# A graph-network layer on one core: B's rows beside zeros, TensorE alone waits for the gathers, and six more groups taken from GpSimd

## The chip, the core and the metric

The kernel runs on one core of a Trainium2 chip. The time is device microseconds of one launch; the median of three runs of the kernel before is 3400.61 us (3400.22 to 3402.1). The engines are called as in the profile: PE (TensorE, with PEld for its weight loads), DVE (VectorE), ACT (ScalarE), POOL (GpSimd) and SP (SyncE, which here only issues transfers).

## What is computed

One message-passing layer with 12500 nodes of 128 features and 400000 edges with 32 features, sorted by their target node:

```python
h = jnp.maximum(_layernorm(x), 0.0)
m = relu(concat([h[src], h[dst], ea]) @ w1 + b1) @ w2 + b2       # 400000 edges
agg = jax.ops.segment_sum(m, dst, num_segments=12500)
gi = agg @ w_ih + b_ih ; gh = h @ w_hh + b_hh                    # a GRU cell
out = x + (1 - z) * n + z * h
```

## The kernel before

w1 has three parts, so an edge's hidden value is relu(A[src] + B[dst] + ea @ w1c) with A = h @ w1a and B = h @ w1b + b1 made once per node. A and B are tables in DRAM; h stays transposed in SBUF (hT_all). The sum over edges is taken before w2, which is folded into the gates.

The edges lie in tiles of 128. Eight tiles are a group k (391 groups; tile j of half a has number a * 4 + j), and a group is worked in two units u = 2k and u = 2k + 1. Because the edges are sorted by target, the targets of a group lie in two windows of V = 32 nodes, the second SHIFT = 8 nodes after the first.

For a group the kernel needs:

- **G**, the rows A[src] of its 1024 edges: 8 indirect gathers of 128 rows each on POOL (`gather`, L156), into one of GBUFS = 11 buffers. The first RAW = 9 groups gather x instead of A.
- **L**, the left side of a product: one-hots of the targets on 64 partitions and the edge features on the other 64. `fetch` (L563, L566) brings it for two groups at a time by two transfers on SP, six groups ahead, into three buffers; DVE makes the one-hots in place (L575).
- **RW**, the right side: rows 0 to 31 hold the first window's 32 rows of B in the left 128 columns, rows 32 to 63 the second window's in the right 128; the rest of these rows is zeros, written once. Below lies w1c. `window_rows` (L602) brings it by two transfers on SP, four groups ahead, into four buffers.
- **pre** = L times RW on PE (L673), B[dst] + ea @ w1c; **RB** = relu(pre + G) on DVE in one instruction (`add`, L701); **OH**, one-hots of the edges' targets in their window, on DVE (`onehot`, L623); and **seg**, PE's products of OH and RB, which sum the edges of a window (L724).

**Groups without a gather.** POOL does not gather all groups. `SPREAD` names how many groups each other engine takes, and spreads them evenly. On ACT and DVE a group's columns of h are copied one by one out of hT_all: on ACT 1024 copies (L960), on DVE 512 instructions that take two columns each (L967) with 8 copies that put them in order (L972); PE then multiplies by w1a, and ACT makes RB by a relu (L710) instead of DVE's add. On SP a group's 1024 rows of A are fetched by 1024 transfers of 512 bytes into the buffer G_sp (L952). Each engine first loads addresses into registers (L945): 16 at a time on ACT, 32 on DVE and SP. A job is cut into steps (4 rows on SP), and `run_jobs` puts them evenly among the units between the job's start and its end; on SP the first starts at u = 24, a job ends at 2k - 8, and the next starts at 2k + 2.

**Order.** The program is written out by hand and every engine works in that order (`manual_schedule`). In one turn of u: new gathers, for an even u the next window's rows and for every second group the next L, then `stages(u)`, which runs several units ahead: one-hots of the group three ahead, `pre(u + 3)`, `add(u + 2)`; then `seg(u)`. Steps of the jobs are put between (`other`). All transfers of SP stand in one queue in program order; they use eight semaphores in turn, so that a transfer is issued only when the eighth before it has landed.

Every 14 groups (BLOCKS) a block of nodes goes through the GRU gates (`node`), and `batch_product` and `batch_store` make and store the next 448 rows of B.

Of the kernel before, what the change touches and what calls it, by code (L numbers as in the profile page):

```python
# [9 lines left out]
F32 = mybir.dt.float32  # L10
F16 = mybir.dt.float16
I32 = mybir.dt.int32
U8 = mybir.dt.uint8
# [39 lines left out]
PIECE = 128  # L53
STEP = {"act": 4, "dve": 8, "sp": 4}
ROW = 4 * D
SPREAD = {"dve": 27, "act": 28, "sp": 2}
START = {"dve": 14, "act": 4, "sp": 24}
NR = 12672

# [4 lines left out]
def tile_gnn(ctx: ExitStack, tc: tile.TileContext, x, src, srcT, dstT, dstP, eaT, eaP, w1, b1, w2T, b2,  # L64
# [69 lines left out]
    A = dram.tile([N, D], F32, name="A")  # L134
    stats = dram.tile([N, 2], F32, name="stats")
    S = dram.tile([NR, D + 1], F32, name="S")
    B = dram.tile([N, D], F32, name="B")
    B_bytes = B.bitcast(U8).rearrange("n f -> (n f)")

    G = {}  # L140

# [6 lines left out]
    def gather(k):  # L148
        if k >= NP or k in mode:
            return  # L150
        G[k] = gp.tile([128, GRP, 2, D], F32, name="G")
        table = x if k < RAW else A
        for u in (2 * k, 2 * k + 1):
            for t, j, a in unit_tiles(u):
                c, i = divmod(t, CH)
                nc.gpsimd.indirect_dma_start(  # L156
                    out=G[k][:, j, a, :], out_offset=None, in_=table,
                    in_offset=bass.IndirectOffsetOnAxis(ap=src_i[c][:, i:i + 1], axis=0))

    for k in range(RAW):  # L160
        gather(k)
# [2 lines left out]
    RB = [const.tile([128, PAIR, D + 4], F32, name=f"RB{i}") for i in range(2)]  # L164
    for r in RB:
        nc.vector.memset(r[:, :, D:], 1.0)
    OHB = [const.tile([128, GRP, 2, V], F32, name=f"OH{i}") for i in range(6)]
    nc.vector.memset(OHB[0], 0.0)


# [18 lines left out]
    nc.vector.memset(zrow, 0.0)  # L189
    RW = [const.tile([128, 2, D], F32, name=f"RW{i}") for i in range(4)]  # L190
    for r in RW:
        nc.vector.memset(r[0:96, :, :], 0.0)
        nc.vector.memset(r[96:128, :, :], 0.0)


    def bn(pool, xs, P, n):
# [45 lines left out]
    def batch_store(j):  # L242
        if j in bt:
            t, n0 = bt.pop(j), j * BATCH
            rows = min(BATCH, N - n0)
            n = rows // 128
            nc.sync.dma_start(B[n0:n0 + n * 128, :].rearrange("(i p) f -> p i f", p=128), t[:, :n, :])
            if rows % 128:
                nc.sync.dma_start(B[n0 + n * 128:n0 + rows, :], t[:rows % 128, n, :])

    def relu_norm(o, xi, st):
        nc.scalar.activation(o, xi, AF.Relu, bias=st[:, 1:2], scale=st[:, 0:1])
# [39 lines left out]
    def setup(pool):  # L292
        nc.vector.tensor_copy(base_f[:, 1:], base_d)
        nc.vector.memset(base_f[:, 0:1], 0.0)
        nc.vector.tensor_scalar(base_f, base_f, float(LAST), 0.0, op0=ALU.min, op1=ALU.max)
        yield
        nc.vector.tensor_copy(at_f[64:65, 512:512 + NP], base_f)
        nc.vector.tensor_tensor(at_f[64:65, :NP], at_f[64:65, 512:512 + NP], at_f[64:65, :NP], op=ALU.is_gt)
        nc.vector.tensor_reduce(beyond, at_f[64:65, :NP], AX.X, ALU.max)
        yield  # L300
        pm = ps1.tile([128, 512], F32, name="misc")
        nc.tensor.matmul(pm[:, :NP], ones, base_f, start=True, stop=True)
        nc.vector.tensor_copy(base_b[:, :, 0], pm[:, :NP])
        yield
        nc.vector.tensor_scalar(base_b[:, :, 1], pm[:, :NP], float(SHIFT), None, op0=ALU.add)
        for a in range(2):
            s = slice(V * a, V * (a + 1))
            nc.vector.tensor_scalar(node_of[s, :], base_b[s, :, a], place_c[s, :], float(-V * a),
                                    op0=ALU.add, op1=ALU.add)
        for b0, b1_, k0, n, w in groups:  # L310
            nc.vector.tensor_scalar(blk_f[:, b0:b1_], base_f[:, k0:k0 + (b1_ - b0 - 1) * n + 1:n], float(N - w),
                                    None, op0=ALU.min)
        yield
        nc.vector.tensor_copy(blk_i, blk_f)
        nc.vector.memset(off_f, 0.0)
        off_c = pool.tile([128, NB * 16], F32, name="off_c", bufs=1)[:1, :].rearrange("o (b n) -> o b n", n=16)
        yield
        nc.vector.memset(off_c, 0.0)
        nc.vector.tensor_tensor(step_f[:, 1:], blk_f[:, 1:], blk_f[:, :-1], op=ALU.subtract)
        nc.vector.memset(step_f[:, 0:1], float(BW))  # L320
        yield
        for b0, b1_, k0, n, w in groups:
            ks = base_f[:, k0:k0 + (b1_ - b0) * n].rearrange("o (b n) -> o b n", n=n)
            nc.vector.tensor_tensor(off_f[:, b0:b1_, :n], ks,
                                    blk_f[:, b0:b1_, None].to_broadcast([1, b1_ - b0, n]), op=ALU.subtract)
            nc.vector.tensor_scalar(base_i[:, b0:b1_, :n], ks, float(4 * D), None, op0=ALU.mult)
            nc.vector.tensor_scalar(off_c[:, b0:b1_, :n], off_f[:, b0:b1_, :n], float(w - V - SHIFT), 0.0,
                                    op0=ALU.min, op1=ALU.max)
        for b0, b1_ in [(0, 1), (1, NW + 1)] + [(b, b + 1) for b in range(NW + 1, NB)]:
            nc.vector.tensor_scalar(step_c[:, b0:b1_], step_f[:, b0:b1_], float(BLOCKS[max(b0 - 1, 0)][2]),  # L330
                                    float(LEAST[b0]), op0=ALU.min, op1=ALU.max)
        nc.vector.tensor_copy(off_i, off_c)
        yield
        nc.vector.tensor_tensor(off_f, off_f, off_c, op=ALU.not_equal)
        nc.vector.tensor_copy(step_i, step_c)
        nc.vector.tensor_tensor(step_f, step_f, step_c, op=ALU.not_equal)
        yield
        yield
        place(0)
# [249 lines left out]
    def window_rows(k):  # L589
        if k >= NP:  # L590
            return
        b = block(k)
        k0, n, _ = BLOCKS[b]
        if k == k0:
            _, vals = nc.values_load_multi_w_load_instructions(
                base_i[0:1, b, 0:n], engines=[ET.SP], min_val=0, max_val=4 * D * LAST,
                skip_runtime_bounds_check_because="clamped above")
            for i, v in enumerate(vals):
                bases[k + i] = v
        v = bases.pop(k)  # L600
        for a in range(2):
            nc.sync.dma_start(RW[k % 4].bitcast(U8)[V * a:V * (a + 1), a, :],  # L602
                              B_bytes[bass.ds(v + 4 * D * SHIFT * a, 4 * D * V)].rearrange(
                                  "(p f) -> p f", p=V))

    def onehot(k):
        if k >= NP:
            return
        t0, t1 = tiles(k)
        OH[k] = OHB[k % len(OHB)]  # L610
        row = SEGB[((k - 3) // 2 + 1) % 2][:, 256:256 + V]
        for a in range(2) if k == 0 else (None,):
            if a is None:
                o, s = OH[k].rearrange("p j a v -> p a j v"), slice(t0, t1)
                d = dloc[:, s].rearrange("p (a j) -> p a j", a=2)[:, :, :, None]
                shape = [128, 2, GRP, V]
                i = row[:, None, None, :]
            else:
                e = min(t1, (a + 1) * GRP)
                o, d = OH[k][:, :e - a * GRP, a, :], dloc[:, a * GRP:e, None]  # L620
                shape = [128, e - a * GRP, V]
                i = row[:, None, :]
            nc.vector.tensor_tensor(o, d.to_broadcast(shape), i.to_broadcast(shape),  # L623
                                    op=ALU.is_equal)

    def unit(u):
        k, h = divmod(u, 2)
# [59 lines left out]
    def add(u):  # L687
# [15 lines left out]
        if h == 1:  # L703
            PP.pop(k)
            G.pop(k, None)

    def relu(u):
        if u in RT:
            o, p = RT.pop(u)
            nc.scalar.activation(o, p, AF.Relu)  # L710
# [4 lines left out]
    def seg(u):  # L715
        k, h = divmod(u, 2)
        p = SEGB[(k // 2) % 2]
        if h == 0 and k % 2 == 0:
            nc.tensor.matmul(p[:, :D + 1], zrow[:, :128], zrow[:, :D + 1], start=True, stop=False)  # L719
        l = unit_tiles(u)  # L720
        rest = l if h else l + unit_tiles(u + 1)
        for i, (t, j, a) in enumerate(l):
            r0 = 2 * V * (k % 2) + V * a
            nc.tensor.matmul(p[r0:r0 + V, :D + 1], OH[k][:, j, a, :],  # L724
                             RB[k % 2][:, 2 * j + a, :D + 1], start=False,
                             stop=all(b != a for _, _, b in rest[i + 1:]))

# [206 lines left out]
    def one_by_one(m, k):  # L934
# [8 lines left out]
        for e0 in range(0, PAIR * 128, LOAD[m]):  # L943
# [4 lines left out]
            if m == "sp":  # L948
                for i, v in enumerate(vals):
                    e = e0 + i  # L950
                    a, j = divmod(e // 128, GRP)
                    nc.sync.dma_start(rows[e % 128:e % 128 + 1, j, a, :],  # L952
                                      A_bytes[bass.ds(v, ROW)].rearrange("(o f) -> o f", o=1))
                    if i % STEP[m] == STEP[m] - 1:
                        yield
                continue
# [64 lines left out]
    def stages(u):  # L1021
# [8 lines left out]
            onehot(u // 2 + 3)  # L1030
        if u + 4 >= 0:
            raw_turn(u + 4)
        if u + 3 >= 0:
            pre(u + 3)
        if u + 2 >= 0:
# [234 lines left out]
```

## Time and profile before

| what | value |
|---|---|
| median of the runs | 3400.61 us |
| profiled execution | 3403.76 us, its span 3401.8 us |
| busy: PE, DVE, ACT, POOL | 2417.4, 2225.1, 3079.4, 2566.1 us |
| granted clock of TensorE | 0.796 |
| moved by the DMA engines | 335.44 MB, 99 GB/s |
| transfers issued on SP: rows of G_sp, RW, L | 2048, 782, 392 |

Busy time leaves out what an engine's sequencer does: loading registers, waiting for semaphores, issuing transfers. In the groups by line, "idle before" is the engine's idle time ahead of these instructions, and "issue" means that nothing in the profile was waited for. In the waits, a row reads: engine and line, what it waited for, microseconds in total, times, longest. SPq and DVEq are the sequencers of these engines. In the order of time, a row has the start, the time from the first to the last of the instructions merged, and their count.

### The profile page before, as it was taken

To read this page: it belongs to the slowest core of one execution; us is meant where nothing else is said; L and a number is where in the kernel's file an instruction comes from. 1 tells how busy PE (TensorE), PEld (TensorE's weight loads), DVE (VectorE), ACT (ScalarE), POOL (GpSimd) and SP (SyncE) were. 2 spreads that over 40 slices of the span, in tenths; PEclk is the share of its full clock that TensorE was granted. 3 is DMA by queue.
4 is the path that set the end of the run, shared out by engine and by line. 5 is a ranking of instruction groups with operands and counts; after the bars stand their busy time and mean duration, and the time that the engine had idled before them with its cause. 6 is when DMAs were issued, how large, how long until landed. Compare 5 with 4: busy or idle time off the path is not lost. (4 is left out here: it accounts for less than half of the span.)

```text
span 3401.8 us, 88642 instructions
## 1 busy us (share of the span) xinstructions
PE 2417.4 (71%) x13113; PEld 1563.7 (46%) x13113; DVE 2225.1 (65%) x16468; ACT 3079.4 (91%) x29057; POOL 2566.1 (75%) x2678
## 2 busy tenths in 40 slices
PE   7567777777677767776777667676677767766767
PEld 7444444444445444544444444444444434444445
DVE  8556666666676666666666666666666666666665
ACT  7699999999999998999899988988988898898984
POOL 7777777777777777777777777777777777777776
PEclk9777887887887778777877877788777778777878
DMA  6434444434443333343434433443433334343332
GB/s 213 106 88 93 97 100 99 101 94 100 102 98 94 98 99 95 95 101 97 98 93 99 98 94 93 96 96 93 98 93 92 95 94 99 92 97 96 92 92 73
DMA packets 191316, 335.44 MB, mean 99 GB/s; under 512 B 66753, under 2 KB 112384, under 8 KB 190729
## 3 DMA queue, kind: packets, MB, share of 16 engines
q0 software_dynamic: 85408, 175.09, 23.0%
q1 hardware_dynamic: 105177, 154.58, 16.4%
q14 instruction: 478, 3.92, 0.4%
q8 instruction: 109, 1.79, 0.2%
q10 hardware_dynamic: 144, 0.07, 0.0%
HBM read 309.24 MB, written 20.24 MB: 97 GB/s over the span
## 5 line engine op out<-in xcount | busy, mean ns | idle before, releaser
L156 POOL DMA_INDIRECT G<-A,src_i x2600 | 2498.9, 961 | 796.2 <-issue 753.7
L960 ACT COPY HE_act<-hT_all 128x4 uint8 x28672 | 2886.8, 189 | 51.4 <-issue 27.0
L967 DVE SCALAR_TENSOR_TENSOR both<-hT_all 128x4 uint16 x13824 | 1173.4, 153 | 988.5 <-issue 980.7
L673 PE MATMUL pre<-RW,L 128*128 128x256 f32 x3128 | 1132.4, 488 | 229.8 <-DVE RB L701 220.6
L673 PEld LDWEIGHTS pre<-RW,L 128*128 128x128 f32 x3128 | 660.6, 236 | 506.1 <-DVE RB L701 234.0
L724 PE MATMUL seg<-RB,OH 128*32 128x129 f32 x6250 | 603.9, 324 | 380.0 <-DVE RB L701 349.7
L724 PEld LDWEIGHTS seg<-RB,OH 128*32 128x32 f32 x6250 | 333.1, 125 | 820.4 <-DVE RB L701 532.7
L701 DVE CUSTOM_DVE_ANT_0 RB<-pre,G 128x1024 f32<-128x1024 f32 (+1 forms) x326 | 394.5, 1210 | 62.7 <-DMA G<-A,src_i 49.2
L575 DVE TENSOR_SCALAR L<-L,node_of 64x512 f32<-64x512 int32 x382 | 186.7, 489 | 9.7 <-DMA L<-in_dstP 9.4
L719 PE MATMUL seg<-zrow 1*128 1x129 bf16 x196 | 45.3, 231 | 164.4 <-DVE OH L623 164.2
L623 DVE TENSOR_TENSOR OH<-dloc,seg 128x256 f32<-128x256 f16 (+1 forms) x392 | 159.5, 407 | 0.5 <-issue 0.5
L750 PE MATMUL nd<-spot,sums 128*128 128x40 f32 x782 | 116.6, 321 | 1.2 <-DVE sums L733 1.2
L750 PEld LDWEIGHTS nd<-spot,sums 128*128 128x128 f32 x782 | 112.4, 231 | 10.5 <-issue 9.0
L710 ACT ACTIVATE RB<-pre 128x1024 f32<-128x1024 f32 x64 | 65.0, 1015 | 52.4 <-PE pre L684 52.4
L809 ACT ACTIVATE gt<-nd 128x512 f32<-128x512 f32 (+2 forms) x28 | 16.4, 585 | 96.5 <-PE nd L803 96.5
L972 DVE COPY HE_dve<-both 128x512 uint8<-128x512 uint8 x216 | 96.6, 447 | 7.4
L684 PEld LDWEIGHTS pre<-w1a,HE_act 128*128 128x128 f32 x448 | 88.4, 245 | 11.6
L684 PEld LDWEIGHTS pre<-w1a,HE_dve 128*128 128x128 f32 x432 | 87.9, 252 | 12.1
L684 PE MATMUL pre<-w1a,HE_act 128*128 128x128 f32 x448 | 86.4, 327 | 0.0
L684 PE MATMUL pre<-w1a,HE_dve 128*128 128x128 f32 x432 | 85.1, 333 | 0.0
L156 POOL DMA_INDIRECT G<-in_x,src_i x69 | 65.9, 954 | 21.8 <-issue 20.7
L233 PE MATMUL nd<-w1b,hT_all 128*128 128x128 f32 x224 | 45.5, 346 | 43.3 <-DVE xb L835 43.3
(177 smaller groups left out, 1383.9 us busy)
## 6 DMA issues: line engine op xcount, KB each, us to landing
L<-in_dstP SPq DMA_DIRECT2D x195, 256.0 KB
L<-in_eaP SPq DMA_DIRECT2D x195, 256.0 KB
G<-A,src_i POOLq DMA_INDIRECT x2600
G_sp<-A SPq DMA_DIRECT2D x2048, 0.5 KB
RW<-B SPq DMA_DIRECT2D x782, 16.0 KB
xb<-in_x SPq DMA_DIRECT2D x26, 256.0 KB
out<-xb SPq DMA_DIRECT2D x26, 256.0 KB
xs<-in_x SPq DMA_DIRECT2D x11, 512.0 KB
```

Source lines behind the costliest of these rows:

```text
L156: nc.gpsimd.indirect_dma_start(out=G[k][:, j, a, :], out_offset=None, in_=table, in_offset=bass.IndirectOffsetOnAxis(ap=src_i[c][:, i:i + ...
L575: nc.vector.tensor_scalar(o, i, node_of[:, k:k + 1], None, op0=ALU.is_equal)
L623: nc.vector.tensor_tensor(o, d.to_broadcast(shape), i.to_broadcast(shape), op=ALU.is_equal)
L673: nc.tensor.matmul(p[:, 2 * i:2 * i + 2, :], Ls[k // QP][:, c0:c0 + 128], RW[k % 4], start=True, stop=not raw)
L684: nc.tensor.matmul(p[:, 2 * i + a, :], cols, w1a, start=False, stop=n + 1 == len(l) or l[n + 1][1] != j)
L701: nc.vector._custom_dve(TENSOR_ADD_SAT, out=o, in0=p, in1=G[k].rearrange("p j a f -> p (j a) f")[:, c, :], s0=float("inf"), s1=0.0)
L710: nc.scalar.activation(o, p, AF.Relu)
L724: nc.tensor.matmul(p[r0:r0 + V, :D + 1], OH[k][:, j, a, :], RB[k % 2][:, 2 * j + a, :D + 1], start=False, stop=all(b != a for _, _, b in r ...
L750: nc.tensor.matmul(p[:, bass.ds(offs[i], V + SHIFT)], sums[:, slot(b, i), :D], spot[:, i % 2, :], start=False, stop=i == len(offs) - 1)
L960: nc.scalar.copy(he[:, e * 4:e * 4 + 4], column(v))
L967: nc.vector.scalar_tensor_tensor(both[:, (e0 % PIECE + i) // 2, :], column(vals[i + 1]), 256.0, column(vals[i]), op0=ALU.mult, op1=ALU.add)
L972: nc.vector.tensor_copy(he[:, p0 * 4:(p0 + PIECE) * 4].rearrange("p (n c b) -> p n c b", c=2, b=4), both.bitcast(U8).rearrange("p n (b c) ...
```

## The change

Four things change.

1. B in DRAM has 256 columns: a row of B and 128 zeros. One transfer of 64 rows of 1 KB writes RW's first 64 partitions whole: for the first window from the row's start, for the second from the zeros that end the row before, so that the zeros come to the left. Each batch of B is stored with a second transfer for the zeros.
2. DVE's add no longer waits for the gathers. A new step `arrived` gives PE a small product that reads one column of all eight tiles of G; it is declared the fence of the group's gathers (and of SP's rows), and DVE waits for PE. It stands one step ahead of `pre`.
3. One-hots are made for two groups at a time, in three buffers of two groups instead of six of one.
4. ACT takes 29 groups instead of 28, DVE 29 instead of 27, SP 5 instead of 2.

```diff
-SPREAD = {"dve": 27, "act": 28, "sp": 2}
+SPREAD = {"dve": 29, "act": 29, "sp": 5}
...
-    B = dram.tile([N, D], F32, name="B")
-    B_bytes = B.bitcast(U8).rearrange("n f -> (n f)")
+    B = dram.tile([N, 2, D], F32, name="B")
+    B_bytes = B.bitcast(U8).rearrange("n a f -> (n a f)")
...
-                nc.gpsimd.indirect_dma_start(
+                fetched = nc.gpsimd.indirect_dma_start(
                     out=G[k][:, j, a, :], out_offset=None, in_=table,
                     in_offset=bass.IndirectOffsetOnAxis(ap=src_i[c][:, i:i + 1], axis=0))
+                if RAW <= k < NP - 1:
+                    tc.add_to_no_dep_group(f"rows{k}", fetched.ins)
...
-            nc.sync.dma_start(B[n0:n0 + n * 128, :].rearrange("(i p) f -> p i f", p=128), t[:, :n, :])
-            if rows % 128:
-                nc.sync.dma_start(B[n0 + n * 128:n0 + rows, :], t[:rows % 128, n, :])
+            for a, v in ((1, none[:, None, :].to_broadcast([128, n + 1, D])), (0, t)):
+                if n:
+                    nc.sync.dma_start(B[n0:n0 + n * 128, a, :].rearrange("(i p) f -> p i f", p=128), v[:, :n, :])
+                if rows % 128:
+                    nc.sync.dma_start(B[n0 + n * 128:n0 + rows, a, :], v[:rows % 128, n, :])
...
-        for a in range(2):
-            nc.sync.dma_start(RW[k % 4].bitcast(U8)[V * a:V * (a + 1), a, :],
-                              B_bytes[bass.ds(v + 4 * D * SHIFT * a, 4 * D * V)].rearrange(
-                                  "(p f) -> p f", p=V))
+        w = B_bytes[bass.ds(v, 8 * D * (V + SHIFT) - 4 * D)]
+        nc.sync.dma_start(
+            RW[k % 4].bitcast(U8)[0:2 * V, :, :].rearrange("p a f -> p (a f)"),
+            bass.AP(tensor=w.tensor, offset=w.offset,
+                    ap=[[8 * D * SHIFT - 4 * D, 2], [8 * D, V], [1, 8 * D]]))
...
     def onehot(k):
-        if k >= NP:
+        if k >= NP or (k % 2 and k > 1):
             return
...
+    def arrived(u):
+        k, h = divmod(u, 2)
+        if 0 < u < NU and h and k < NP - 1 and u not in HE and k not in hand:
+            p = SEGB[((u - 2) // 4 + 1) % 2][0:1, 320:320 + PAIR]
+            i = nc.tensor.matmul(p, eps, G[k].rearrange("p j a f -> p (j a) f")[:, :, 0], start=True, stop=True)
+            tc.declare_fence(i.ins, group=f"rows{k}")
...
+        arrived(u + 2)
         if u + 3 >= 0:
             pre(u + 3)
```

More of the change, by code (lines that the diff above doesn't have):

```diff
@@ L166, in tile_gnn @@
         nc.vector.memset(r[:, :, D:], 1.0)
-    OHB = [const.tile([128, GRP, 2, V], F32, name=f"OH{i}") for i in range(6)]
+    OHB = [const.tile([128, 2 * PAIR, V], F32, name=f"OH{i}") for i in range(3)]
     nc.vector.memset(OHB[0], 0.0)
@@ L191, in tile_gnn @@
     for r in RW:
-        nc.vector.memset(r[0:96, :, :], 0.0)
+        nc.vector.memset(r[64:96, :, :], 0.0)
         nc.vector.memset(r[96:128, :, :], 0.0)
+    none = const.tile([128, D], F32, name="none")
+    nc.vector.memset(none, 0.0)
     def bn(pool, xs, P, n):
@@ L325, in setup @@
                                     blk_f[:, b0:b1_, None].to_broadcast([1, b1_ - b0, n]), op=ALU.subtract)
-            nc.vector.tensor_scalar(base_i[:, b0:b1_, :n], ks, float(4 * D), None, op0=ALU.mult)
+            nc.vector.tensor_scalar(base_i[:, b0:b1_, :n], ks, float(8 * D), None, op0=ALU.mult)
             nc.vector.tensor_scalar(off_c[:, b0:b1_, :n], off_f[:, b0:b1_, :n], float(w - V - SHIFT), 0.0,
@@ L595, in window_rows @@
             _, vals = nc.values_load_multi_w_load_instructions(
-                base_i[0:1, b, 0:n], engines=[ET.SP], min_val=0, max_val=4 * D * LAST,
+                base_i[0:1, b, 0:n], engines=[ET.SP], min_val=0, max_val=8 * D * LAST,
                 skip_runtime_bounds_check_because="clamped above")
@@ L600, in window_rows @@
         v = bases.pop(k)
-        for a in range(2):
-            nc.sync.dma_start(RW[k % 4].bitcast(U8)[V * a:V * (a + 1), a, :],
-                              B_bytes[bass.ds(v + 4 * D * SHIFT * a, 4 * D * V)].rearrange(
-                                  "(p f) -> p f", p=V))
+        w = B_bytes[bass.ds(v, 8 * D * (V + SHIFT) - 4 * D)]
[3 more added lines that the diff above has]
+                    ap=[[8 * D * SHIFT - 4 * D, 2], [8 * D, V], [1, 8 * D]]))
     def onehot(k):
-        if k >= NP:
+        if k >= NP or (k % 2 and k > 1):
             return
-        t0, t1 = tiles(k)
-        OH[k] = OHB[k % len(OHB)]
+        o = OHB[(k // 2) % len(OHB)]
         row = SEGB[((k - 3) // 2 + 1) % 2][:, 256:256 + V]
[L612 to L624, printed above, removed]
+        n = 2 if 1 < k < NP - 1 else 1
+        for i in range(n):
+            OH[k + i] = o[:, PAIR * ((k + i) % 2):PAIR * ((k + i) % 2) + PAIR, :]
+        t0, t1 = tiles(k)[0], tiles(k + n - 1)[1]
+        if k:
+            parts = ((o[:, PAIR * (k % 2):PAIR * (k % 2) + t1 - t0, :], t0, t1),)
+        else:
+            parts = tuple((OH[0][:, a * GRP:min(t1, (a + 1) * GRP), :], a * GRP, min(t1, (a + 1) * GRP))
+                          for a in range(2))
+        for p, e0, e1 in parts:
+            shape = [128, e1 - e0, V]
+            nc.vector.tensor_tensor(p, dloc[:, e0:e1, None].to_broadcast(shape),
+                                    row[:, None, :].to_broadcast(shape), op=ALU.is_equal)
     def unit(u):
@@ L723, in seg @@
             r0 = 2 * V * (k % 2) + V * a
-            nc.tensor.matmul(p[r0:r0 + V, :D + 1], OH[k][:, j, a, :],
+            nc.tensor.matmul(p[r0:r0 + V, :D + 1], OH[k][:, a * GRP + j, :],
                              RB[k % 2][:, 2 * j + a, :D + 1], start=False,
@@ L951, in one_by_one @@
                     a, j = divmod(e // 128, GRP)
-                    nc.sync.dma_start(rows[e % 128:e % 128 + 1, j, a, :],
+                    fetched = nc.sync.dma_start(rows[e % 128:e % 128 + 1, j, a, :],
                                       A_bytes[bass.ds(v, ROW)].rearrange("(o f) -> o f", o=1))
+                    tc.add_to_no_dep_group(f"rows{k}", fetched.ins)
                     if i % STEP[m] == STEP[m] - 1:
```

## The prediction

> **What bounds the kernel now.** I read the page first (busy times, costliest groups), then the groups by line, then the waits of every engine, last the order of time on SP's queue.
>
> ```profile
> span 3401.8 us, 88642 instructions
> PE 2417.4 (71%) x13113; PEld 1563.7 (46%) x13113; DVE 2225.1 (65%) x16468; ACT 3079.4 (91%) x29057; POOL 2566.1 (75%) x2678
> L960 ACT COPY HE_act<-hT_all 128x4 uint8 x28672 | 2886.8, 189 | 51.4 <-issue 27.0
> L156 POOL DMA_INDIRECT G<-A,src_i x2600 | 2498.9, 961 | 796.2 <-issue 753.7 <-DMA G<-A,src_i 19.5 <-DVE both L967 5.5
> L967 DVE SCALAR_TENSOR_TENSOR both<-hT_all 128x4 uint16 x13824 | 1173.4, 153 | 988.5 <-issue 980.7 <-DMA G_sp<-A 5.2
> L701 DVE CUSTOM_DVE_ANT_0 RB<-pre,G 128x1024 f32<-128x1024 f32 (+1 forms) x326 | 394.5, 1210 | 62.7 <-DMA G<-A,src_i 49.2 <-PE pre L673 11.6 <-issue 1.6
> ```
>
> POOL issues gathers from end to end: one costs (2498.9 + 796.2) / 2600 = 1.267 us, and of the 796.2 us idle, 753.7 are its own issue; hardly any of it is a wait. 2669 gathers (2600 and the first 69) make 3382 us, so POOL sets the time. DVE is close behind: 2225.1 busy and 980.7 in which it starves while its own sequencer loads addresses, together 3206. ACT, with 3079.4, is as close. So far the kernel looks like one that gains from taking gathers off POOL.
>
> The fourth supplier has no busy share on the page, because SP only issues. Its waits tell how much room it has:
>
> ```profile
> SPq L952 <- DMA L<-in_dstP: 865.4, 150, 8.1
> SPq L563 <- PE pre L673: 233.9, 63, 14.1
> SPq L602 <- DMA L<-in_dstP: 90.3, 16, 6.9
> SPq L563 <- PE pre L684: 87.0, 13, 13.2
> SPq L602 <- PE pre L673: 73.0, 23, 9.2
> ```
>
> Two kinds must be kept apart. Where SP waits for PE (233.9 + 87.0 + 73.0 = 394 us), it has run ahead to the end of the L and RW buffers: that is slack. Where it waits for the transfer of L (865.4 + 90.3 and smaller ones), it is held by its own queue, whatever the rest does: that is cost. SP's own demand is therefore about 3402 - 394 = 3008 us of 3402. How the cost arises is seen in the order of time, one round of two groups, from one L to the next:
>
> ```profile
> 1522.74 0.81 SPq L602 DMA_DIRECT2D RW<-B  x2
> 1523.67 0.60 SPq L563 DMA_DIRECT2D L<-in_dstP  x1
> 1524.32 0.50 SPq L566 DMA_DIRECT2D L<-in_eaP  x1
> 1524.93 10.48 SPq L952 DMA_DIRECT2D G_sp<-A  x8
> 1535.51 0.84 SPq L602 DMA_DIRECT2D RW<-B  x2
> 1536.45 1.21 SPq L952 DMA_DIRECT2D G_sp<-A  x4
> 1537.82 0.81 SPq L602 DMA_DIRECT2D RW<-B  x2
> 1538.93 0.57 SPq L563 DMA_DIRECT2D L<-in_dstP  x1
> ```
> ```profile
> 1534.30 1.12 SPq L952 DMA_DIRECT2D G_sp<-A  x2
> ```
>
> (The second fence is the same time in a closer window.) The program gives SP's transfers eight semaphores in turn, so each waits for the eighth before it. L goes out at 1523.67, its partner next, then six rows of G_sp; the seventh waits until L has landed and goes at 1534.30, 10.6 us after L. No more than six short transfers fit in that hole, however many are queued behind. The round takes 15.26 us; the kernel needs 3401.8 / 195.5 = 17.4 us per round.
>
> **The change, part by part.**
>
> *Three more groups on SP (2 to 5).* Each is 1024 one-row transfers and 32 loads of addresses:
>
> ```profile
> L952 SPq DMA_DIRECT2D G_sp<-A x2048: 224/228/643, 229.9 to 3276.4; - x187
> L945 SPq TENSOR_LOAD <-at x64: 1876/2142/2377, 227.6 to 3229.5; - x64
> L602 SPq DMA_DIRECT2D RW<-B x782: 315/321/1530, 99.4 to 3366.2; - x196
> ```
> ```profile
> L<-in_dstP SPq DMA_DIRECT2D x195, 256.0 KB
> RW<-B SPq DMA_DIRECT2D x782, 16.0 KB
> B<-xb SPq DMA_DIRECT2D x25, 192.0 KB
> B<-xb SPq DMA_DIRECT2D x24, 32.0 KB
> ```
>
> Four rows took 1.21 us at 1536.45, so they follow each other by (1.21 - 0.23) / 3 = 0.33 us. 3072 of them make 1014 us, 96 loads of 2.14 us make 205. By the program's spreading the five jobs lie one behind another from u = 24 to u = 750, 142 and four times 136 units long, so a loaded unit has 1024 / 136 = 7.5 rows instead of 3, a round 30 instead of 12. Six of the 30 fit in the hole behind L; the rest stands on SP's own path. Queued behind them on SP are the window's rows (RW, four buffers) and L (three): PE's product of the next group waits for these.
>
> *B beside zeros, one transfer for a group's 64 rows.* 391 issues fewer; two took 0.81 us, so one and its gap are 0.41: -160 us on SP. The zeros are stored with each batch: the 49 issues of B<-xb and 6 of B<-bt double, 55 more at 0.4 us make 22 us, and the data follow them on the same queue. A group moves 64 KB instead of 32 KB, 12.8 MB in all.
>
> Whether the larger transfer holds the queue longer, the trace doesn't show. From one side: it lands as the present ones and costs nothing; from the other: it moves as L does, whose 256 KB took 10.6 us, so 64 KB take 2.6 us. If every L waits behind that, 172 loaded rounds add 450 us. I take nothing, since RW and L differ fourfold in size and RW is nearest to itself, and keep the 450 for the range. The Trainium skill, "DMA: Bandwidth & Descriptors", section on why a DMA increments its semaphore by 16, says that a DMA uses the largest number of engines up to 16 that divides the slowest dimension on both sides. The new source has a slowest dimension of 2, as L's from dstP has, where a present RW transfer has 32; by that rule the costly side would hold, and the sum would be up to 4540 instead of 4090. L's 10.6 us agrees with it without proving it.
>
> *Six groups off POOL.* Where a job is hand-made, its 8 gathers go: 48 x 1.267 = -61 us, on the path now. Without anything else in the way the end comes at 3402 - 61 = 3341.
>
> *DVE.*
>
> ```profile
> L972 DVE COPY HE_dve<-both 128x512 uint8<-128x512 uint8 x216 | 96.6, 447 | 7.4
> L623 DVE TENSOR_TENSOR OH<-dloc,seg 128x256 f32<-128x256 f16 (+1 forms) x392 | 159.5, 407 | 0.5 <-issue 0.5
> L813 DVE TENSOR_TENSOR gt<-gt,misc 128x512 f32<-128x512 f32 (+2 forms) x28 | 18.6, 666 | 1.3 <-PE misc L801 1.2
> L701 DVEq EVENT_SEMAPHORE  x1358: 21/50/2846, 201.2 to 3386.5; - x194
> ```
>
> Two groups more: (1173.4 + 988.5 + 96.6) / 27 = 83.6 us each, +167. One-hots of two groups: 392 of 0.407 become about 197 of the size of the 666 ns row, 131 us instead of 159: -28. Three groups fewer have the add of 1.21 us: -4. The waits for gathers, 1358 of 50 ns, leave its sequencer: between -68 (if all were in the open) and 0 (if queued work covers them). DVE's 3206 becomes 3273 to 3341, plus the waits that remain of its 190 us: some 3340 to 3500. That alone could take back the 61 us.
>
> *ACT.* One group is 2886.8 / 28 = 103 us, and three more groups end in a relu:
>
> ```profile
> L710 ACT ACTIVATE RB<-pre 128x1024 f32<-128x1024 f32 x64 | 65.0, 1015 | 52.4 <-PE pre L684 52.4
> L673 PE MATMUL pre<-RW,L 128*128 128x256 f32 x3128 | 1132.4, 488 | 229.8 <-DVE RB L701 220.6 <-DMA RW<-B 9.2
> L755 PEld LDWEIGHTS <-dcol 128*128 128x128 f16 x382 | 32.7, 106 | 56.7 <-DVE dcol L780 46.8 <-issue 4.5 <-DVE both L967 1.1
> ```
>
> 3079 + 103 + 3 = 3185 us of work, under 3341.
>
> *PE alone waits for gathers.* 323 groups get a product of 8 columns. Bounds: 0.1 us (the weight load of L755) to 0.49 us (a product of L673 with 256 columns), 32 to 158 us of PE, which idles 984 us; nothing on the path. Behind the waiting product stand pre of the next group and seg of the last; a late gather now holds both, where it held DVE's add alone. DVE waited 49.2 us for gathers in all, which bounds this. In SP's regime below gathers are early.
>
> **The sum.** SP: 3402 - 394 + 1014 + 205 - 160 + 22 = 4089 us. It exceeds POOL's 3341, ACT's and DVE's, so SP sets the time, and what the others save is hidden. Check by rounds: 15.26 + 18 x 0.33 - 2 x 0.41 + 30/32 x 2.14 = 22.4 us in 172 loaded rounds is 3850, and 48 unloaded groups at 8.7 us add 418: 4270. That round is one of the slower ones, so I stay with the total. The hole behind L, on average (865.4 + 90.3) / 195 = 4.9 us now, can grow to the 7 us seen here: +360 at most. It can shrink if fewer gathers per us let L land earlier; I put this at a tenth of 10.6 us, -180, an estimate without a row. I take neither. The profiled execution took 3403.76 us, 2 more than its span and 3 more than the median; 4089 + 2 - 3 is about 4090.
>
> **The rivals.**
> - *L is held back by the larger RW.* The two-row source speaks for it, the size against it: 4300 to 4540.
> - *The hole shrinks, SP is less over-full.* If L landed in 7 us, 172 rounds give back 3.6 us each: 3470; half of that 3780. Against it: the largest waits are 8.1 us, and L's size and form are unchanged. 3500 to 3950.
> - *SP keeps up and POOL's saving is paid out: faster.* It holds if SP's 4089 drop under 3341, 748 us of the 956 that it spends waiting behind L. For it: POOL is at 1.267 us with no waits, so each gather saved is time saved. 3341, up to 3390 with some of DVE's waits.
> - *SP keeps up, DVE sets the pace.* It holds if DVE's sequencer gains nothing from the 1358 waits: 3400 to 3480, no gain or a small loss.
>
> **How the numbers follow.** SP with L as it is (3950 to 4300): 60%. L held back by RW: 12%. Hole shrinks: 10%. POOL's saving paid out: 13%. DVE's pace: 5%, of which 2 lie within 0.2% of before (7 us, about what a measurement here tells from no change) and 3 above. So faster 13%, same 2%, slower 85%. 3600 to 4500 leaves out the last two cases and little else.
>
> **What would show it.** SP's waits for PE at L and RW fall from 394 us to a few tens, and its waits behind L stay near 1000. From one L to the next pass 20 to 23 us. PE's product (pre<-RW,L) and DVE's L line wait for RW and L by hundreds of us, where now it is 9; POOL's gaps become waits for a G buffer. The prediction is wrong if SP still waits for PE by hundreds of us, if the seventh row behind L goes out in 5 us or less, or if rows of G_sp follow each other in under 0.2 us.

## The result, and the profile after

| | before | changed |
|---|---|---|
| median of 4 runs | 3401.36 us | 4645.5 us |
| profiled execution | 3403.76 us | 4637.15 us |
| ratio, 95% interval | | 1.365 (1.3601 to 1.3699) |

The changed kernel is 36.5% slower. The direction and the engine that sets the time were forecast; 4090 us and the range to 4500 were too low.

Rows from the page of the changed kernel (busy times, then some of the groups: busy, mean ns, idle ahead of them and its releaser):

```profile
span 4635.4 us, 97025 instructions
PE 2669.2 (58%) x13807; PEld 1697.2 (37%) x13807; DVE 2328.6 (50%) x17312; ACT 3197.2 (69%) x30084; POOL 2508.9 (54%) x2630
L156 POOL DMA_INDIRECT G<-A,src_i x2552 | 2441.8, 957 | 1988.4 <-DVE RB L707 1257.8
L679 PE MATMUL pre<-RW,L 128*128 128x256 f32 x3128 | 1285.0, 543 | 869.0 <-DMA RW<-B 679.3
L717 PE MATMUL seg<-G,eps 128*1 128x8 f32 x636 | 64.1, 175 | 1002.1 <-DVE OH L629 893.8
L581 DVE TENSOR_SCALAR L<-L,node_of 64x512 f32<-64x512 int32 x382 | 185.7, 486 | 643.4 <-DMA L<-in_dstP 640.7
```

POOL, which hardly waited before, now stands 1258 us for buffers that DVE's add hasn't freed. DVE waits 641 us for L, PE 679 us for RW: both come from SP. SP's own waits in the changed kernel:

```profile
SPq L965 <- DMA L<-in_dstP: 1122.8, 172, 9.0
SPq L965 <- DMA RW<-B: 182.4, 233, 1.7
SPq L569 <- PE pre L679: 97.9, 25, 12.3
SPq L965 <- DMA L<-in_eaP: 83.8, 171, 1.5
...
SPq L608 <- PE pre L690: 41.2, 7, 10.0
SPq L608 <- PE pre L679: 29.3, 18, 8.5
SPq L569 <- PE pre L690: 28.5, 4, 12.5
```

Its slack, the waits for PE, has fallen from 394 us to 197. What it loses in its own queue has grown, and a row stands there that was absent before: G_sp waits for RW (182 us). One round in the order of time, and the seventh row behind L in a closer window:

```profile
2016.03 0.64 SPq L608 DMA_DIRECT2D RW<-B  x1
2016.79 0.53 SPq L569 DMA_DIRECT2D L<-in_dstP  x1
2017.37 0.54 SPq L572 DMA_DIRECT2D L<-in_eaP  x1
2018.02 12.52 SPq L965 DMA_DIRECT2D G_sp<-A  x16
2030.63 0.57 SPq L608 DMA_DIRECT2D RW<-B  x1
2031.26 0.43 SPq L119 DMA_DIRECT2D dst_i<-in_dstT  x1
2033.92 3.83 SPq L965 DMA_DIRECT2D G_sp<-A  x12
2037.92 0.56 SPq L608 DMA_DIRECT2D RW<-B  x1
2038.58 0.52 SPq L569 DMA_DIRECT2D L<-in_dstP  x1
```
```profile
2027.22 3.00 SPq L965 DMA_DIRECT2D G_sp<-A  x9
```

The seventh row goes out 10.4 us after L (10.6 before), and the round takes 21.8 us. The forecast shape is there. (This round is one of the faster ones: the mean over the kernel is 4635.4 / 195.5 = 23.7 us.) But PE's small product (L717) also stood 1002 us, nearly all for DVE's one-hots: a wait that the prediction didn't have at all, and that could be a second cause or only an effect of the first. The experiments had to tell this, and to size the parts. TensorE's granted clock is lower too, 0.728 against 0.796, and the 3128 products of L and RW are 153 us longer in all (1285.0 against 1132.4). PE stood idle for 1871 us ahead of these products and the small ones, so that may cost nothing, but no run holds the clock fixed.

### The profile page after: what moved, and what is told of

Its sections match the earlier page's. It is cut to its first block, busy times and chain, and to the rows that moved or that the text cites. A ratio compares the mean times of both kernels' runs of the same rounds, so it can differ in the third digit from the quotient of the medians.

```text
span 4635.4 us, 97025 instructions
## 1 busy us (share of the span) xinstructions
PE 2669.2 (58%) x13807; PEld 1697.2 (37%) x13807; DVE 2328.6 (50%) x17312; ACT 3197.2 (69%) x30084; POOL 2508.9 (54%) x2630
## 5 line engine op out<-in xcount | busy, mean ns | idle before, releaser
L156 POOL DMA_INDIRECT G<-A,src_i x2552 | 2441.8, 957 | 1988.4 <-DVE RB L707 1257.8
L974 ACT COPY HE_act<-hT_all 128x4 uint8 x29696 | 2995.5, 189 | 61.9 <-issue 34.7
L981 DVE SCALAR_TENSOR_TENSOR both<-hT_all 128x4 uint16 x14848 | 1248.6, 153 | 1255.2 <-issue 1235.6
L679 PE MATMUL pre<-RW,L 128*128 128x256 f32 x3128 | 1285.0, 543 | 869.0 <-DMA RW<-B 679.3
L679 PEld LDWEIGHTS pre<-RW,L 128*128 128x128 f32 x3128 | 741.4, 265 | 1115.7 <-issue 1003.9
L737 PE MATMUL seg<-RB,OH 128*32 128x129 f32 x6250 | 638.0, 338 | 18.0 <-ACT RB L723 17.4
L717 PE MATMUL seg<-G,eps 128*1 128x8 f32 x636 | 64.1, 175 | 1002.1 <-DVE OH L629 893.8
L717 PEld LDWEIGHTS seg<-G,eps 128*1 128x1 f32 x636 | 33.5, 82 | 1096.9 <-DVE OH L629 952.2
L629 DVE TENSOR_TENSOR OH<-dloc,seg 128x512 f32<-128x512 f16 (+1 forms) x198 | 132.3, 669 | 0.0
L746 DVE COPY sums<-seg 128x129 f32<-128x129 f32 x196 | 55.5, 283 | 57.6 <-PE seg L737 57.4
```

The costliest lines, as they stand in the source:

```text
L156: fetched = nc.gpsimd.indirect_dma_start(out=G[k][:, j, a, :], out_offset=None, in_=table, in_offset=bass.IndirectOffsetOnAxis(ap=src_i[c] ...
L629: nc.vector.tensor_tensor(p, dloc[:, e0:e1, None].to_broadcast(shape), row[:, None, :].to_broadcast(shape), op=ALU.is_equal)
L679: nc.tensor.matmul(p[:, 2 * i:2 * i + 2, :], Ls[k // QP][:, c0:c0 + 128], RW[k % 4], start=True, stop=not raw)
L717: i = nc.tensor.matmul(p, eps, G[k].rearrange("p j a f -> p (j a) f")[:, :, 0], start=True, stop=True)
L737: nc.tensor.matmul(p[r0:r0 + V, :D + 1], OH[k][:, a * GRP + j, :], RB[k % 2][:, 2 * j + a, :D + 1], start=False, stop=all(b != a for _, _, ...
L974: nc.scalar.copy(he[:, e * 4:e * 4 + 4], column(v))
```

## The experiments

Run beside the experiments, the kernel before took 3398 to 3406 us (medians of seven executions each); each run is held against the median beside it. "One execution" marks a run with a single time. Differences between runs are taken from their times, also where these come from different chips, on which the kernel before agreed to 0.3%.

**SP's rows alone.** The kernel before, with three more groups on SP:

```diff
-SPREAD = {"dve": 27, "act": 28, "sp": 2}
+SPREAD = {"dve": 27, "act": 28, "sp": 5}
```

> The kernel before with SP's groups at 5 and nothing else changed (ACT 28, DVE 27). Queue theory: SP is over-full by the rows alone, 4300 to 4500 us. Rival (the new form of RW is the main cost): SP's issue fits better without it, under 4100 us. Rival (PE's new wait): no such wait here, about 3340 to 3450 us.

4350 us (one execution). SP's waits in it, behind L and for PE:

```profile
SPq L952 <- DMA L<-in_dstP: 982.6, 174, 7.8
...
SPq L602 <- PE pre L673: 53.7, 15, 10.7
SPq L563 <- PE pre L673: 52.2, 25, 9.2
SPq L563 <- PE pre L684: 41.3, 6, 12.1
```

Its demand is 4348 - 147 = 4201 us; the prediction's own terms for this case, 3008 + 1014 + 205, make 4227. The three groups alone account for some 950 of the 1244 us, with no product for the gathers on PE and no new RW in the program.

**The form of RW.** The changed kernel with B and RW as before (two transfers of 32 rows of 512 bytes):

```diff
-        nc.sync.dma_start(RW[...][0:2 * V, :, :], bass.AP(..., ap=[[8 * D * SHIFT - 4 * D, 2], [8 * D, V], [1, 8 * D]]))
+        for a in range(2):
+            nc.sync.dma_start(RW[...][V * a:V * (a + 1), a, :], B_bytes[bass.ds(v + 4 * D * SHIFT * a, 4 * D * V)]...)
```

> The changed kernel with B as before and RW in two transfers of 32 rows of 512 bytes, SP at 5. If the one transfer of 64 KB holds SP's queue (its two-row source as slow as L's), undoing it gives back the waits for RW and about 1 us of L's landing in each round and costs 0.2 us of issue per group: 4400 to 4520 us, and the waits of G_sp for RW (182 us) vanish. If the transfer's form costs nothing, the extra issues make it slower than 4645: 4650 to 4750 us.

4374 us (one execution), somewhat under the range expected if the form holds the queue, and far from the other. It is 271 us faster than the changed kernel, although it issues 391 transfers more for RW. To tell the source's form from its doubled bytes, the same 64 rows of 1 KB were then brought by two transfers of 32 rows each:

```diff
+        for a in range(2):
+            w = B_bytes[bass.ds(v + (8 * D * SHIFT - 4 * D) * a, 8 * D * V)]
+            nc.sync.dma_start(RW[...][V * a:V * a + V, :, :]..., w.rearrange("(p f) -> p f", p=V))
```

> The changed kernel, SP at 5, with the same 64 rows of 1 KB brought into RW by two transfers of 32 rows instead of one of two times 32 (the kernel of e9, on another chip). If the two-row source is what makes the one transfer slow: as e3, 4350 to 4420 us, with G_sp's waits for RW gone. If the bytes (64 KB instead of 32 KB for a group) are what costs: 4640 to 4750 us, since issues are added.

4406 us (one execution). G_sp's waits for RW fell from 182.4 us to 0.5, and those behind L from 1122.8 to 950.3. SP's longest waits are:

```profile
SPq L965 <- DMA L<-in_dstP: 950.3, 170, 7.8
SPq L965 <- DMA L<-in_eaP: 92.4, 170, 1.5
SPq L569 <- PE pre L679: 83.7, 24, 12.1
```

So some 240 of the 271 us come from moving the 64 rows as one transfer with a two-row source. The other 30 are left for the bytes and the stores of zeros, but e3 and e9b have a single execution each, on different chips, so that share is not shown. The one transfer also takes longer to issue than one of the two:

```profile
L608 SPq DMA_DIRECT2D RW<-B x391: 519/577/6517, 101.3 to 4599.0; - x196
```

0.577 us (median) against 0.321 for each of the two before: the change saved little on the issue and lost more in the queue.

**The hole behind L.** The changed kernel, SP at 5, with L's targets in two transfers, each of one row of dstP copied to 32 partitions:

```diff
-        p = dstP[:, c]
-        nc.sync.dma_start(Ls[q][:2 * V, ...], bass.AP(..., ap=[list(p.ap[0]), [0, V], [1, n * 512]]))
+        for a in range(2):
+            p = dstP[a:a + 1, c]
+            nc.sync.dma_start(Ls[q][V * a:V * a + V, ...], bass.AP(..., ap=[[0, V], [1, n * 512]]))
```

> The changed kernel, SP at 5, with L's targets fetched by two transfers, one for each row of dstP copied to 32 partitions, instead of one transfer with a two-row source. Queue theory: L lands in 3 to 5 us instead of 11, the hole behind it closes, 1100 us of SP's waiting go and 110 us of issue are added: 3450 to 3700 us. Rival (the rows' issue alone is the bound, the hole only fills otherwise idle time): 4400 us or more. Rival (PE's new wait): 4400 us or more.

3826 us, 1.123 times before (1.1211 to 1.1256), and 819 less than the changed kernel. In the order of time 16 rows behind L now take 8.00 us instead of 12.52, and the wait for L's targets is 64 us instead of 1123:

```profile
2014.97 0.85 SPq L570 DMA_DIRECT2D L<-in_dstP  x2
2015.87 0.55 SPq L573 DMA_DIRECT2D L<-in_eaP  x1
2016.54 8.00 SPq L966 DMA_DIRECT2D G_sp<-A  x16
```
```profile
SPq L966 <- DMA RW<-B: 304.6, 241, 2.5
SPq L570 <- PE pre L680: 156.2, 25, 13.0
SPq L966 <- DMA L<-in_eaP: 121.2, 155, 1.5
SPq L966 <- DMA L<-in_dstP: 64.0, 192, 1.0
```

The halves are smaller than the one transfer, but size alone doesn't explain it: the eighth row here waits for L's other part (L573), still one transfer of 256 KB, whose slowest dimension is its 64 rows, and it goes out at 2021.75, so that part had landed within 5.9 us of its issue, where the two-row transfer of the same size held the seventh row for 10.4. The hole was the larger part of SP's cost, as the queue theory says. But the time ends above the 3450 to 3700 expected: something else sets it there.

**What lies under SP.** The changed kernel with SP's groups back at 2:

```diff
-SPREAD = {"dve": 29, "act": 29, "sp": 5}
+SPREAD = {"dve": 29, "act": 29, "sp": 2}
```

> The changed kernel with SP's groups back at 2 (ACT and DVE stay at 29), all else as changed. Queue theory (SP's rows and the hole behind L set the time): SP's demand falls by three groups of 415 to 560 us each, from 4440 to 2750 to 3190, under POOL's 2645 gathers of 1.267 us; 3350 to 3470 us. Rival (PE's new wait for the gathers holds the products behind it and is what costs): the wait is the same for every group, so at least 3900 us.

3774 us, 1.1085 times before (1.1066 to 1.1103). Both theories miss: 871 us go, so SP is the cause of most; some 370 us stay, so it is not the cause of all. PE's small product and DVE in this run:

```profile
L717 PE MATMUL seg<-G,eps 128*1 128x8 f32 x642 | 64.4, 175 | 1082.1 <-DVE OH L629 688.6 <-DVE sums L746 372.6 <-DMA G_sp<-A 7.2
L981 DVE SCALAR_TENSOR_TENSOR both<-hT_all 128x4 uint16 x14848 | 1256.2, 154 | 1186.4 <-issue 1174.0 <-DMA RW<-B 3.6 <-DMA G_sp<-A 3.5
L707 DVE CUSTOM_DVE_ANT_0 RB<-pre,G 128x1024 f32<-128x1024 f32 x323 | 393.2, 1218 | 120.7 <-PE seg L717 108.6 <-PE seg L737 8.3 <-issue 1.5
```

The product hardly waits for a gather (7 us). It waits 1061 us for DVE's one-hots and sums, which read other columns of the tile `seg` into which it writes. PE is thus stopped each time until DVE has come to its one-hots, and DVE's add then waits for PE. Three runs test this; the first two have ACT 29, DVE 29 and SP 2, as this one. First, without the product, DVE waiting for the gathers itself (both gathers and SP's rows leave the group that the product fenced):

```diff
-                    tc.add_to_no_dep_group(f"rows{k}", fetched.ins)
...
-        arrived(u + 2)
```

> As e1_sp2 (ACT 29, DVE 29, SP 2), but without PE's product for the gathers: DVE's add waits for them itself again. Bank theory (PE's small product is written into the seg bank, and waits there for DVE's one-hots and sums, 1070 us in e1, so that PE goes in step with DVE and DVE's add then waits for PE): those waits go, DVE starves as long per group as before (29/27 of 980 = 1053 us instead of 1174) and its add no longer waits 109 us for PE: 3440 to 3560 us. Rival (29 groups are too many for DVE, whoever waits): 3650 us or more.

3579 us (1.0525; 1.0503 to 1.0547), 195 less, a little above the expected range. Second, the product as it is, but written into the tile `pre` of the next group, which the next product overwrites:

```diff
             PP[k] = ps2.tile([128, PAIR, D], F32, name="pre")
+            arrived(u - 1, PP[k][0:1, 0, 0:PAIR])
...
-            p = SEGB[((u - 2) // 4 + 1) % 2][0:1, 320:320 + PAIR]
```

> As e1_sp2, but PE's small product is written into the pre tile that the next product overwrites, not into the seg bank. Bank theory: PE waits for DVE as little as before, DVE has no waits for gathers: 3400 to 3550 us. Rival (a PE that waits for the gathers in order is the cost, wherever it writes): 3650 us or more.

3501 us (1.0297; 1.0276 to 1.0317), 273 less than with the seg tile. DVE's add no longer waits for PE to speak of, and DVE starves about as long per group as in the kernel before (1072 / 29 = 37 us, against 981 / 27 = 36):

```profile
L981 DVE SCALAR_TENSOR_TENSOR both<-hT_all 128x4 uint16 x14848 | 1252.0, 153 | 1082.0 <-issue 1072.2 <-DMA G_sp<-A 3.7 <-DMA RW<-B 3.4
L708 DVE CUSTOM_DVE_ANT_0 RB<-pre,G 128x1024 f32<-128x1024 f32 x323 | 390.4, 1209 | 14.8 <-PE pre L717 13.8 <-PE pre L680 0.9
100.00:3400.00 3300.00, 2361.87 (x13041) 1521.19 (x13043) 2173.33 (x16698) 3079.95 (x29545) 2469.21 (x2571) 0.78 0.39 100
```

(The last row is the stretch from 100 to 3400 us: after the length, busy time and count of PE, PEld, DVE, ACT, POOL.) So PE's waiting for gathers is not what cost; the place that its product writes was. With the right place it is worth 78 us against DVE's own waiting (3579 - 3501). What remains over 3400 is put down to DVE: in this stretch 2173 us busy and 1062 starved fill 3235 of the 3300. Third, the edits without the six groups:

```diff
-SPREAD = {"dve": 29, "act": 29, "sp": 5}
+SPREAD = {"dve": 27, "act": 28, "sp": 2}
```

> The changed kernel with the spread of before (ACT 28, DVE 27, SP 2): the edits without the six groups. If DVE's total is the bound in e1 (2321 busy, 1174 starved, some 260 waiting), two groups fewer give back 2 x 84 to 90 us: 3590 to 3610 us, still 5% slower than before. If the edits alone cost nothing and only the groups do: 3390 to 3420 us.

3586 us (1.0545; 1.0524 to 1.0567), 4 under the range expected: the edits alone, as written, are 5.5% slower, and the two groups on DVE (with one on ACT) cost 188 us, 94 for each of DVE's.

**Repairs.** If these parts are all of it, a kernel without them must fall to POOL's pace. First the kernel before, with L in two transfers and two groups more on SP:

```diff
-SPREAD = {"dve": 27, "act": 28, "sp": 2}
+SPREAD = {"dve": 27, "act": 28, "sp": 4}
...
```

> The kernel before with L's targets in two transfers of 32 copied rows each, and SP at 4 (ACT 28, DVE 27). If the hole behind L is what fills SP, its demand is 3008 - 956 + 100 + 2 x 415 = 2980 us, SP keeps up, and POOL's 2653 gathers set the time: 3361 + 18 = 3380 us, 0.6% faster. If the hole is only time in which SP had nothing to do, SP is over-full: 3008 + 2 x 415 = 3840 us.

3378 us, 0.993 times before (0.9913 to 0.9946). Then all repairs together: L and RW in two transfers each, PE's product in `pre`, one-hots by pairs, and DVE's groups back at 27:

```diff
-SPREAD = {"dve": 29, "act": 29, "sp": 5}
+SPREAD = {"dve": 27, "act": 29, "sp": 4}
...
```

> All repairs together (the kernel of e10, on another chip): PE's product for the gathers in the pre tile, RW in two transfers of 512-byte rows, L's targets in two transfers, one-hots of two groups as changed; ACT 29, DVE 27, SP 4. POOL's 2645 gathers make 3351 + 18 = 3369 us if it sets the pace; DVE's demand is 3492 - 2 x 85 = 3322, ACT's 3354 and a few tens, SP's about 3065. Expected 3365 to 3385 us. If ACT at 29 is too much beside the products that it waits for: 3400 us or more.

3366 us, 0.9909 times before (0.9892 to 0.9926): 0.9% faster than the kernel before, and the fastest here. POOL's period is (2470.6 + 787.3) / 2576 = 1.265 us, with hardly a wait; its 2645 gathers make 3346 us of it:

```profile
L156 POOL DMA_INDIRECT G<-A,src_i x2576 | 2470.6, 959 | 787.3 <-issue 747.9 <-DMA G<-A,src_i 17.4 <-DVE both L979 6.4
```

The same with SP at 5:

> The same with SP at 5 (the kernel of e11): POOL's 2637 gathers would allow 3359 us, and SP's demand, 3587 in the run with L spread less 305 of waits for RW plus 200 for RW's second issue, is 3480. If demand as added up here holds, 3450 to 3550 us; if SP can hide more, about 3360.

3425 us (1.008; 1.0057 to 1.0104), some 25 us under the range expected. PE waits for SP again, and POOL, still without waits, starts its last gather 82 us before the end, where it was 18:

```profile
PE pre L678 <- DMA RW<-B: 548.2, 181, 8.7
```

Even with both holes closed, five groups are more than SP can issue: from 300 to 3200 us SP waits for PE's products only 31 us in all, against 321 in the run before.

## Why the prediction was right and wrong

- *SP becomes the bound: right.* It was read from the waits, where an engine without busy time shows its room. For the rows alone the terms hold to 1%, and not by errors that cancel: 4227 forecast, 4201 measured as demand in e2, and SP's waits for L's targets over all its lines are 1016 us there against 1045 before.
- *SP's slack is used up: wrong by 197 us.* The sum took off all of the 394 us. The units before the first job, the gaps between jobs and the tail still leave SP ahead of PE: of the 197 us, 91 lie before 300 us, 51 after 4400, and only 55 between. This comes near a sign of being wrong that the prediction named, SP still waiting for PE by hundreds of us. The time is the demand plus this rest, so a sum of SP's demand alone is low by that rest: some 150 of the missed 555 us (e2: 4201 + 147 = 4348).
- *RW in one transfer: the term that failed.* It was put at -160 us of issue, +22 for the zeros, and nothing for the queue. Undoing it gives 271 us, so the term was wrong by some 410. The reason given, that RW is nearest to itself, was the mistake: the row nearest to the new form was L's, the other transfer with a two-row source. The bound of 450 for this term was wide enough; the chance of 12% was far too small, and with the rest of the point before added, 4645 lies above even this rival's 4540. The rule of the Trainium skill, "DMA: Bandwidth & Descriptors", section on why a DMA increments its semaphore by 16, says that the slowest dimension limits the number of engines. The runs agree: the same bytes in the same rows cost 4406 us with a slowest dimension of 32 and 4645 with 2, and L's targets, taken from 2 to 32, let SP's wait fall from 1123 to 64 us. On how many engines a transfer ran, no trace here shows.
- *PE's product costs nothing on the path: wrong, though SP hid it.* Counted were its length and the gathers that it waits for, both rightly small. Not counted was the tile it writes. Under SP's bound it changes little (e2 and e3, without and with it and three more groups on DVE and ACT, lie at 4350 and 4374); once SP has room it is 273 us (e1 to e6). So the rival "SP keeps up, POOL's saving is paid out" had no chance with this program: e1, where SP does keep up, is 3774. The Trainium skill, "PSUM — Partial Sum Buffer", section "PSUM bank collisions raise a hardware error", asks to guard PSUM by bank and quadrant, not by address; the product writes columns 320 to 327 and the one-hots read columns 256 to 287 of one bank (the tile `seg` lies in PSUM). The trace shows that the program holds PE back there; no run here shows a collision itself.
- *DVE: 3340 to 3500 if it had the pace.* With the product out of the way (e6) it has it, at 3501, 1 us over the upper end. The 84 us per group hold there, (1252.0 + 1082.0 + 104.7) / 29 = 84 (with the product in the seg tile a group cost 94), and so do the 28 us for the one-hots (669 ns against 666 assumed). DVE's other waits make up the rest.
- *The hole behind L, put at no change: right for the rows alone.* In e2 G_sp's rows wait 982.6 us there against 865.4, but other transfers wait less, and the total is that of before (1016 against 1045). With the new RW in the queue the total is 1129: that growth belongs to the term that failed.
- *What would show it.* PE and DVE wait for RW and L by 679 and 641 us, rounds take 21.8 us, POOL waits for buffers: as said. SP's waits for PE fell to 197, not to "a few tens", and the mean round of 23.7 us lies above the 20 to 23.

## What to carry to other kernels

An engine that only issues has no busy share, so read its room from its waits: those for other engines are slack, those for its own transfers are cost, and a job of many small transfers is priced with the holes that a large one tears into the same queue. When a transfer is reshaped, compare it with the transfer in the trace that has the same outer dimension, not with its former self. A product made only to wait for something still needs a place to write: put it in the tile that its engine is about to overwrite; here, in another tile, it waited 1061 us for that tile's readers.

## What was not expected of the hardware

One transfer of 64 rows took 0.577 us to issue where one of 32 took 0.321, with rows of 512 bytes (before) and of 1 KB (e9b) alike, so joining two saved 0.065 us of issue, not half. And three kernels (e9b, e10b and e11b) had first been run on another chip, on which the kernel before took 5664 us; in the repaired kernel with SP at 4 there, ACT's copies were as long as ever (190 ns), but ACT stood 2131.6 us for nothing that the profile shows, where it is 28.3 here:

```profile
L972 ACT COPY HE_act<-hT_all 128x4 uint8 x29696 | 3268.2, 190 | 2158.9 <-issue 2131.6 <-DVE bn L204 0.3
```

The ratio there was 1.0255 (1.0232 to 1.0279) for the kernel that is 0.9909 here, and 1.0292 (1.0252 to 1.0332) for the one with SP at 5 that is 1.008; the kernel that takes 4406 us here took 5648 there (one execution), no longer than the kernel before. So a rank order of such kernels on one chip need not hold on another. The cause wasn't found.
